# An eight-layer network on one core: layer 6 regrouped into 64-token chunks, weights centred ahead, attention's sums placed earlier in TensorE's queue

## The chip, the cores and the metric

The kernel runs on one core of a Trainium2 chip. The metric is the device time of one execution in microseconds (us). The core has five engines with a queue of instructions each: PE (TensorE, matmuls; PEld is its weight load), DVE (VectorE), ACT (ScalarE), POOL (GpSimd) and SP (SyncE, which issues DMAs). Each queue is worked off in order.

## What is computed

The reference takes `x` of 4 sequences x 1024 tokens x 128 columns through eight layers. After each, `x = layernorm(x + layer(x))`, without weight or bias:

```python
def _layernorm(x, axis=-1, eps=1e-05):
    m = jnp.mean(x, axis=axis, keepdims=True)
    v = jnp.var(x, axis=axis, keepdims=True)
    return (x - m) / jnp.sqrt(v + eps)
```

Layers 0 to 7 are: a similarity count with a linear map `W2` (0); a binarised feed-forward (1); attention in which, for every token and each of 16 heads, the 64 queries of the head attend to its 64 keys under a causal mask (2); a ternary feed-forward with an inner layer norm (3); a gated linear recurrence (4); four routed experts (5); a state-space layer (6); two Kronecker mixtures of experts with top-2 routing (7). Two of them matter here.

Layer 2, for each token and head, `softmax(mask(q k^T)) v` over 64 x 64 scores: by far the most elementwise work.

Layer 6 (16 heads, state 64, head width 8) works in chunks, and any chunk length gives the same result. With `A` the log decay of a token, `B` and `C` projections of 64 columns per head, `X` the scaled input:

```python
Lmat = jnp.exp(segsum(A))
Y_diag = jnp.einsum('bclhn,bcshn,bhcls,bcshp->bclhp', C, B, Lmat, X)
states = jnp.einsum('bclhn,bhcl,bclhp->bchpn', B, decay_states, X)
Y_off = jnp.einsum('bclhn,bchpn,bhcl->bclhp', C, states, state_decay_out)
```

## The kernel before

**Tiling and stages.** The 4096 tokens are 32 tiles of 128 tokens on the partitions. Layers 0 and 1 (`front`, line 1824) run over eight blocks of four tiles. Layer 2 runs over 64 units of 64 tokens, two per tile. Layers 3 to 7 run over nine groups (`SIZES`, line 27): seven of four tiles, two of two.

**Layer 2.** `prepare` (795) makes queries and masked maxima, `feed` (862) cuts each unit into 17 pieces of 128 to 1920 columns, and `rest` (917) finishes a piece. A piece goes round all engines: DVE multiplies queries by a key (903; two of the 17 on POOL), POOL subtracts the maximum (931), ACT exponentiates, PE adds up the denominators `den` (949), DVE multiplies in place by the value (954), PE adds up the numerators `num` (966). Pieces in flight lie in a ring of `ERING` = 8904 columns (line 33). `close` (986) divides (`rd<-num`, 992), and after each second unit multiplies by `Wo`, adds the residual and normalises the tile.

**Norms.** `norm` (549) ends layers 0, 1, 3, 4, 5 and 6: DVE adds the residual in PSUM (lines 635, 735, 1112, 1224, 1539; layer 5 adds it with its experts), `stats` (534) takes bn_stats and bn_aggr per tile on DVE, ACT makes the reciprocal deviation, and `shifts` (563) the shift; ACT then scales and shifts each tile, and `transpose` (572) turns it on PE. `close` has its own copy of this for one tile, whose last step is on DVE.

**Layer 6** (1313): per group, for each tile `j` and each quarter `hq` of the heads, `chunk` (1406) projects `B` and `C` of four heads into one bank, lays them in SBUF, makes the decay rows `em` (four ACT passes of 128 columns, a sum on PE in float32, an Exp), multiplies them with the products `C B` on DVE (two of 256 columns), and adds `X` weighted by them into the output bank (`within`, 1425). `across` (1460) adds the old state's part, transposes `B`, makes the new state's increment and updates the state on DVE (two of 8 columns). 128 such chunks in all. `drain` (1497) gates the output.

**Order.** All of it is one program in which a planner sets the order. Each stage is a generator that yields the engine it needs next; `Order.note` (173) adds up estimated durations (`length`, 85) and `Order.run` (249) always takes the step that can start first. Among steps of one engine that start within 0.05 us of each other, the rank decides (`URGE`, 1934, in `urge`, 240): `close` 0, `prepare` 1, the chains of the other layers 2, `rest` 3, `feed` 4; a chain that is ahead of the attention's pace gets 9. When attention is through, its rooms (ring, PSUM banks, query buffers) are handed to the other layers by `retire` (354) and the list `HEIRS` (1931). Every operation is recorded in one helper, so the profile shows line 61 for all; they are told apart by tile names.

The rank is read here:

```python
URGE = {"close": 0, "prepare": 1, "chain_a": 2, "chain_b": 2, "chain_c": 2, "rest": 3, "feed": 4}
```

Of the kernel before, what the change touches and what calls it, by code (L numbers as in the profile page):

```python
# [32 lines left out]
ERING = 8904  # L33
# [6 lines left out]
    "f2_bu": 1, "a3_bdt": 16, "a3_Alog": 16, "f3_sup": 1, "f3_sdn": 1, "bup": 64, "bdn": 32, "rep": 32, "SL": P, "U": P,  # L40
# [98 lines left out]
class Order:  # L139
# [100 lines left out]
    def urge(self, t):  # L240

        if t.rank in self.pace:
            group, steps, size = self.pace[t.rank]
            lag, total = LAG[t.rank]
            if group + size * min(1.0, steps / total) > self.place - (lag if group < HURRY else 0.0):
                return 9
        return self.rank[t.rank]
# [73 lines left out]
class Model:  # L321
# [4 lines left out]
    def __init__(self, ctx, tc, a):  # L326
# [13 lines left out]
            "x": (5, 512), "xT": (5, 512), "a": (6, 512), "b": (12, 512), "c": (4, 512), "gt": (1, 1024), "xp": (2, 152),  # L340
# [79 lines left out]
    def start(self):  # L420
# [23 lines left out]
        for i in range(3):  # L444
            self.d.dma_start(left[32 * i : 32 * i + 2], a["bias"])
        for i in range(3):
            self.v.tensor_copy(part, left[:66])
            self.v.tensor_copy(self.bias[32 * i : 32 * i + 2], part[32 * i : 32 * i + 2])
            self.v.tensor_tensor(left[:66], left[:66], part, ALU.subtract)
# [4 lines left out]
        self.d.dma_start(self.Wo, a["a1_Wo"].rearrange("(c p) d -> p c d", p=P))  # L454

# [7 lines left out]
        self.state = self.keep([P, 8, 32], "state")  # L463
# [3 lines left out]
        self.negA = self.keep([P, H], "negA")  # L467
# [5 lines left out]
        self.mask16 = self.keep([P, P], "mask16", dtype=BF16)  # L473
        self.v.tensor_scalar(self.mask16, self.k["SL"], -30000.0, None, ALU.mult)
# [73 lines left out]

    def norm(self, g, c, r):

        x = g.x
        mv, rs = yield from self.stats(r, c)
        nm = self.shifts(c, mv, rs)
        for j in range(g.n):
            self.s.activation(x[:, j, :], r[:, j, :], AF.Identity, scale=rs[:, j : j + 1], bias=nm[:, j : j + 1])
        self.drop(r)
        yield from self.transpose(g.xT, [x[:, j, :] for j in range(g.n)])
# [50 lines left out]
    def count(self, g, nT):  # L608
# [18 lines left out]
        w = yield from self.load("a", self.a["a0_W2"].rearrange("(c p) d -> p c d", p=P), 2, D)  # L627
# [6 lines left out]
        yield "DVE"  # L634
        self.v.tensor_tensor(po, g.x, po, ALU.add)
# [23 lines left out]
    def binarise(self):  # L659

        for half, n, count in ((0, 1, D), (1, 4, 512)):
# [22 lines left out]
            self.v.tensor_tensor(wT, wT, bw, ALU.add)  # L684
            self.drop(ab, bw, alpha)
# [4 lines left out]
            self.drop(wT)  # L690

# [17 lines left out]
    def layer1(self, g):  # L709
# [15 lines left out]
        for j in range(TPG):  # L725
# [3 lines left out]
            for f in range(4):  # L729
                self.pe.matmul(  # L730
                    po[:, j, :], lhsT=hT[:, f, j * P : (j + 1) * P], rhs=w2T[:, f * D : (f + 1) * D],
                    start=False, stop=(f == 3),
                )
        yield "DVE"
        self.v.tensor_tensor(po, g.x, po, ALU.add)
# [250 lines left out]
    def close(self, unit):  # L986
# [22 lines left out]
        if u == 1:  # L1009
# [10 lines left out]
            st, mv, rs = self.small([P, 6], "cst"), self.small([P, 2], "cmv"), self.small([P, 1], "crs")  # L1020
            self.v.tensor_tensor(po, x, po, ALU.add)
            self.v.bn_stats(st, po)
            self.v.bn_aggr(mv, st)
            yield "ACT"
            self.rstd(rs, mv[:, 1:2])
            yield "DVE"
            self.v.tensor_scalar(x, po, mv[:, 0:1], rs, ALU.subtract, ALU.mult)
# [10 lines left out]
    def ternarise(self):  # L1038
        self.w3 = []
        for half in range(2):  # L1040
# [18 lines left out]
            self.v.scalar_tensor_tensor(wT, wT, hi, neg, ALU.is_gt, ALU.subtract)  # L1059
            self.drop(pg, neg)  # L1060
# [5 lines left out]
    def layer3(self, g):  # L1066
# [37 lines left out]
        for j in range(n):  # L1104
            yield "PE"
            for f in range(4):
                self.pe.matmul(
                    po[:, j, :], lhsT=hT[f][:, j * P : (j + 1) * P], rhs=prT[:, f * D : (f + 1) * D],
                    start=(f == 0), stop=(f == 3),
                )  # L1110
        yield "DVE"
        self.v.tensor_tensor(po, g.x, po, ALU.add)
# [5 lines left out]
    def layer4(self, g):  # L1118
# [89 lines left out]
        Wo = yield from self.load("a", a["a2_Wo"], D)  # L1208
# [12 lines left out]
        for j in range(n):  # L1221
            self.pe.matmul(po[:, j, :], lhsT=og[:, j * P : (j + 1) * P], rhs=Wo, start=True, stop=True)
        yield "DVE"
        self.v.tensor_tensor(po, g.x, po, ALU.add)
# [4 lines left out]
    def layer5(self, g):  # L1229
# [4 lines left out]
        def fetch(e):  # L1234
# [3 lines left out]
            self.d.dma_start(ew[e][1], a["f2_W2"][512 * e : 512 * e + 512].rearrange("(c p) d -> p c d", p=P))  # L1238
# [74 lines left out]
    def layer6(self, g):  # L1313
        a, xT, n = self.a, g.xT, g.n
        SL, U = self.k["SL"], self.k["U"]
        yield "SP", self.free("b", 2)
        w, room = self.new("b"), self.new("b")
        X = room[:, : n * D].rearrange("p (j h q) -> p j h q", h=H, q=8)
        wbcs = {}

        def weights():
            for hq in range(4):
                yield "SP", self.free("b", 1 if n == TPG else 6)
                wbcs[hq] = self.new("b")
                for i, name in enumerate(("WB", "WC")):
                    self.d.dma_start(wbcs[hq][:, 256 * i : 256 * i + 256], a["a3_" + name][:, 256 * hq : 256 * hq + 256])
# [3 lines left out]
        self.d.dma_start(Wout, a["a3_Wout"])  # L1330
        Xf = X.rearrange("p j h q -> p j (h q)")

        little = room[:, n * D : n * D + 40 * n] if n < TPG else self.small([P, 40 * n], "little", bufs=1)
        dt, A = (little[:, 16 * n * i : 16 * n * (i + 1)].rearrange("p (j h) -> p j h", h=H) for i in range(2))
        over = little[:, 32 * n :].rearrange("p (j e) -> p j e", e=8)
# [5 lines left out]
        def inner(j):  # L1341
            yield "PE", self.free("bg")
            ps = self.new("bg")
            self.pe.matmul(ps[:, :144], lhsT=xT[:, j * P : (j + 1) * P], rhs=Wx, start=True, stop=True)
            yield "ACT"
            self.s.copy(Xf[:, j, :], ps[:, :D])
            yield "DVE"
            self.v.tensor_tensor(dt[:, j, :], ps[:, D : D + H], self.k["a3_bdt"], ALU.add)
            self.drop(ps)

        yield from self.together(*(inner(j) for j in range(n)))
        yield "ACT", self.free("bg")
        ps = self.new("bg")[:, : 2 * n * H].rearrange("p (i j h) -> p i j h", i=2, h=H)
# [3 lines left out]
        self.v.tensor_tensor(A, dt, self.negA[:, None, :].to_broadcast([P, n, H]), ALU.mult)  # L1357
        yield "DVE"
        self.v.tensor_tensor(X, X, dt[:, :, :, None].to_broadcast([P, n, H, 8]), ALU.mult)
# [4 lines left out]
        pa = ps[:, : 2 * n * H].rearrange("p (i j h) -> p i j h", i=2, h=H)  # L1364
        for i, m in enumerate((SL, self.ones)):
# [5 lines left out]
        for e in range(2):  # L1371
            rows = slice(64 * e, 64 * e + 64)
            self.s.activation(over[rows], pa[rows, 1].rearrange("p j (t e) -> p j t e", e=2)[:, :, :, e], AF.Exp)
        if n == TPG:
            dx = self.small([P, n, H, 8], "dx", bufs=1)
            yield "DVE"
        else:
            yield "DVE", self.free("b", 4)
            dx = self.new("b", n, H, 8)
        self.v.tensor_tensor(dx, X, pa[:, 0, :, :, None].to_broadcast([P, n, H, 8]), ALU.mult)  # L1380
# [18 lines left out]
        def add(t, jj, what, i, lhsT, rhs):  # L1399
            sums, done = bank(t)  # L1400
            done[i] += 1
            self.pe.matmul(
                sums[32 * i : 32 * i + 32, jj, what, :], lhsT=lhsT, rhs=rhs, start=done[i] == 1, stop=done[i] == 16
            )

        def chunk(j, hq):
            cols, at, hs = slice(j * P, (j + 1) * P), 4 * j + hq, slice(4 * hq, 4 * hq + 4)

            yield "PE", self.free(
                "bg", also=lambda: count["begun"] == at and hq in wbcs and min(moved) >= j - 1,  # L1410
                at=lambda: self.order.until(wbcs[hq]), b=3,
            )
            count["begun"] += 1
            bc, em, ps = self.new("b", 4, P), self.new("b", 4, P), self.new("bg", 4, P)
            wbc = wbcs[hq].rearrange("p (i c) -> p i c", c=P)
            for i in range(4):
# [641 lines left out]
```

## Time and profile before

| | |
|---|---|
| median of 3 runs | 3943.88 us (3942.16 to 3946.77) |
| the profiled execution | 3950.88 us |
| its span, first to last instruction | 3949.1 us |
| mean granted TensorE clock | 0.912 |
| chain that ended last, by engine | DVE 27%, PE 26%, POOL 15%, ACT 15%, issue 11%, DMA 5% |
| DMA | 331.30 MB, mean 84 GB/s |

A line of a group of instructions reads: engine, operation, output tile <- input tiles, shapes (partitions x elements), count | busy us, mean ns of one | idle us of the engine just before them, and what ended it. A line of waits reads: engine and tile that waited <- engine and tile that released it: us in total, times, longest. A window's line has its length and then each engine's busy us with its instructions.

### The profile page before, as it was taken

The numbers are of one execution on the slowest core, as the hardware profiler recorded it, in microseconds if no ns is written. First come the engines' busy times: TensorE is split into PE (matmuls) and PEld (weight loads), VectorE is DVE, ScalarE is ACT, GpSimd is POOL, SyncE is SP. The second block draws the span as 40 slices with busy tenths as digits, with TensorE's granted clock in tenths as the row PEclk, the third lists the DMA queues.
The fourth block names the chain that finished last, engine by engine and source line by source line (L and its number), as shares of the span: only waits on it lengthen the run. The fifth ranks groups of instructions, "written<-read, shape, count | busy, mean of one in ns | idle before, by whom it ended". The sixth has DMA issues, their size and how long they took to land.

```text
span 3949.1 us, 128735 instructions
## 1 busy us (share of the span) xinstructions
PE 3099.8 (78%) x55472; PEld 1614.1 (41%) x55472; DVE 3258.2 (83%) x4477; ACT 2612.3 (66%) x4970; POOL 2921.3 (74%) x1320
## 2 busy tenths in 40 slices
PE   6676677777788887978888887887878887879883
PEld 2232223333344453544444543544434443436562
DVE  3878999899998879989988789999998998893421
ACT  5576575666677785677667775777657776666541
POOL 1879996899789777879778787798888986791000
PEclk8788888988999998999999999999999999999986
DMA  3221222212224134233433324343432334234565
GB/s 90 58 50 44 47 64 53 60 44 49 52 66 115 51 90 105 66 109 83 100 84 79 101 63 97 80 121 79 101 75 62 105 81 122 71 86 117 163 154 118
DMA packets 385297, 331.30 MB, mean 84 GB/s; under 512 B 196108, under 2 KB 320460, under 8 KB 384728
## 3 DMA queue, kind: packets, MB, share of 16 engines
q1 hardware_dynamic: 375384, 289.53, 29.6%
q0 software_dynamic: 9344, 33.56, 2.9%
q8 instruction: 434, 7.11, 0.8%
q14 instruction: 135, 1.11, 0.1%
HBM read 147.85 MB, written 40.89 MB: 48 GB/s over the span
## 4 chain that ended last, share of the span: by engine, by line
DVE 27%; PE 26%; POOL 15%; ACT 15%; issue 11%; DMA 5%; SPq 1%; DVEq 0%; POOLq 0%; ACTq 0%
DVE ringe L61 17%; POOL ringe L61 15%; PE bg L61 14%; ACT ringe L61 7%; PE den L61 6%; DVE bg L61 5%; PE num L61 4%; PE kvr L61 2%; ACT b L61 1%; ACT ha L61 1%; SPq L61 1%; ACT L61 1%; DVE a L61 1%; DVE b L61 1%; ACT t L61 1%
## 5 line engine op out<-in xcount | busy, mean ns | idle before, releaser
L61 POOL TENSOR_TENSOR ringe<-ringe,mr 128x1024 f32<-128x1024 f32 (+14 forms) x1088 | 2557.1, 2384 | 459.1 <-DVE ringe L61 342.5
L61 DVE TENSOR_TENSOR ringe<-ringe,kvr 128x1024 f32<-128x1024 f32 (+14 forms) x1094 | 1288.0, 1207 | 188.8 <-PE den L61 168.0
L61 ACT ACTIVATE ringe<-ringe 128x768 f32<-128x768 f32 (+14 forms) x962 | 999.5, 1056 | 580.5 <-POOL ringe L61 578.6
L61 DVE TENSOR_TENSOR ringe<-qr,kvr 128x1024 f32<-128x1024 f32 (+12 forms) x960 | 1102.0, 1184 | 33.9 <-PE num L61 24.5
L61 PE MATMUL den<-ringe,cst 128*32 128x256 f32 (+7 forms) x8712 | 697.8, 416 | 263.7 <-ACT ringe L61 230.0
L61 PE MATMUL num<-ringe,cst 128*32 128x256 f32 (+7 forms) x8712 | 698.6, 407 | 245.8 <-DVE ringe L61 239.3
L61 PEld LDWEIGHTS num<-ringe,cst 128*32 128x32 f32 x8712 | 227.1, 113 | 585.9 <-DVE ringe L61 458.3
L61 PEld LDWEIGHTS den<-ringe,cst 128*32 128x32 f32 x8712 | 232.9, 114 | 571.5 <-ACT ringe L61 365.5
L61 ACT ACTIVATE ringe<-ringe,cst 128x256 f32<-128x256 f32 x512 | 357.4, 781 | 60.9 <-POOL ringe L61 60.8
L61 POOL TENSOR_TENSOR ringe<-qr,ks 128x896 f32<-128x896 f32 (+1 forms) x128 | 286.9, 2241 | 88.3 <-PE num L61 66.0
L61 PE MATMUL bg<-xT,a 128*32 128x512 f32 (+1 forms) x1868 | 249.4, 629 | 30.5 <-DVE a L61 12.1
L61 PE MATMUL kvr<-wkv,xT 128*32 128x256 f32 x2048 | 148.9, 412 | 35.7 <-DVE ringe L61 31.0
L61 DVE TENSOR_TENSOR_SCAN bg<-ends,bg 128x512 f32<-128x512 bf16 x128 | 155.1, 1216 | 25.2 <-PE bg L61 25.2
L61 PE MATMUL bg<-a,ha 128*32 128x128 f32 x4672 | 164.4, 285 | 13.7 <-ACT ha L61 13.7
L61 ACT COPY b<-bg 128x256 f32<-128x256 f32 (+2 forms) x224 | 99.6, 452 | 94.3 <-PE bg L61 82.2
L61 PEld LDWEIGHTS bg<-a,ha 128*32 128x32 f32 x4672 | 131.0, 115 | 35.0 <-ACT ha L61 17.5
L61 PE MATMUL bg<-xT,b 128*32 128x128 f32 (+1 forms) x3448 | 127.8, 290 | 6.4 <-DVE state L61 3.5
L61 ACT ACTIVATE b<-cst,little 128x128 f32<-128x128 f32 x416 | 132.0, 395 | 0.0
L61 DVE TENSOR_TENSOR b<-b,bg 128x256 f32<-128x256 f32 (+1 forms) x252 | 97.4, 419 | 27.6 <-PE bg L61 22.9
L61 ACT ACTIVATE ha<-bg,cst 128x512 f32<-128x512 f32 (+1 forms) x152 | 98.8, 674 | 31.8 <-PE bg L61 30.5
L61 PE MATMUL bg<-b,cst 128*32 128x512 f32 x864 | 116.7, 606 | 1.8 <-ACT b L61 1.4
L61 PEld LDWEIGHTS bg<-xT,b 128*32 128x32 f32 x3448 | 102.4, 115 | 36.2 <-issue 17.1
(681 smaller groups left out, 4405.2 us busy)
## 6 DMA issues: line engine op xcount, KB each, us to landing
qr<-q SPq DMA_DIRECT2D x512, 128.0 KB
mr<-t SPq DMA_DIRECT2D x512, 128.0 KB
a<-in_f_W SPq DMA_DIRECT2D x65, 256.0 KB
c<-in_f_Wdn SPq DMA_DIRECT2D x54, 256.0 KB
c<-tu SPq DMA_DIRECT2D x196, 64.0 KB
tu<-gt SPq DMA_DIRECT2D x24, 512.0 KB
c<-td SPq DMA_DIRECT2D x92, 128.0 KB
td<-gt SPq DMA_DIRECT2D x22, 512.0 KB
```

Of the source, the lines that this page charges most:

```text
L61: return f(*args, **kw)
```

## The change

- **Layer 6** takes chunks of 64 tokens. The two halves of the partitions hold two heads (even and odd, by a reordering of the weights on the host), so a tile of 128 tokens is two chunks `c` with two heads `e`; `chunk(j, b)` now covers eight heads, and 64 of them make the layer. `B` and `C` have a bank each. The products, the transposition (a matmul by the identity), the increments, the old state's part and the outputs are matmuls on 64 x 64 or 64 x 32 corners of the array, sixteen of each per chunk. The decay rows are eight ACT passes of 64 columns, the decay product is one DVE instruction of 512 columns, and the state is updated twice per chunk, by a multiplication and an addition of 32 columns each.
- **Centred weights.** `centre` takes from each row of a final weight its mean over the 128 outputs, so that a layer's output has mean zero (`x` has it already). It is applied once to the weights and biases that end layers 0 to 6; those that are loaded again and again go to DRAM and back (`levelled`). A norm is then only a scaling: `level` squares on ACT with an accumulator and scales on ACT. The residual comes in by a matmul with the identity (by an identity in `W2` in layer 0); in `close` and layer 5 DVE still adds it.
- **Order**: `rest` on PE, that is the sums `den` and `num`, has the rank of `prepare`.
- **Rooms**: the ring has 8368 columns, `xp` 448 instead of 152, `state` 56 per head pair instead of 32.

```diff
-ERING = 8904
+ERING = 8368
...
+        if t.rank == "rest" and t.engine == "PE":
+            return self.rank["prepare"]
         return self.rank[t.rank]
...
+    def centre(self, w, n):
+
+        rows = w.partition_size()
+        w = w.rearrange("p (c d) -> p c d", c=n)
+        s = self.small([P, 8], "mean", bufs=1)[:rows, :n]
+        self.v.tensor_reduce(s, w, AX.X, ALU.add)
+        self.v.tensor_scalar_mul(s, s, 1.0 / D)
+        self.v.tensor_tensor(w, w, s[:, :, None].to_broadcast([rows, n, D]), ALU.subtract)
+
+    def level(self, x, r, rs):
+
+        n = r.shape[1]
+        for j in range(n):
+            self.s.activation(x[:, j, :], r[:, j, :], AF.Square, accum_out=rs[:, j : j + 1])
+        self.s.activation(rs, rs, AF.Ln, scale=1.0 / D, bias=self.eps)
+        self.s.activation(rs, rs, AF.Exp, scale=-0.5)
+        for j in range(n):
+            self.s.activation(x[:, j, :], r[:, j, :], AF.Copy, scale=rs[:, j : j + 1])
+
     def norm(self, g, c, r):
 
-        x = g.x
-        mv, rs = yield from self.stats(r, c)
-        nm = self.shifts(c, mv, rs)
-        for j in range(g.n):
-            self.s.activation(x[:, j, :], r[:, j, :], AF.Identity, scale=rs[:, j : j + 1], bias=nm[:, j : j + 1])
+        x, rs = g.x, self.small([P, TPG], c + "rs")[:, : g.n]
+        yield "ACT"
+        self.level(x, r, rs)
...
-        w = yield from self.load("a", self.a["a0_W2"].rearrange("(c p) d -> p c d", p=P), 2, D)
+        w = yield from self.load("a", self.level_w["a0_W2"][0], 2, D)
...
+    def levelled(self, *names):
+
+        for name in names:
+            src = self.a[name].rearrange("(e c p) d -> e p c d", p=P, c=min(4, self.a[name].shape[0] // P))
+            self.level_w[name] = []
+            for e in range(src.shape[0]):
+                n = src.shape[2]
+                w = yield from self.load("a", src[e], n, D)
+                yield "DVE"
+                if name == "a0_W2":
+                    self.v.tensor_tensor(w[:, 0, :], w[:, 0, :], self.ident, ALU.add)
+                self.centre(w.rearrange("p c d -> p (c d)"), n)
+                yield "SP"
+                put_by = self.keep([P, n * D], name, pool=self.dram)
+                self.d.dma_start(put_by, w.rearrange("p c d -> p (c d)"))
+                self.level_w[name].append(put_by)
+                self.drop(w)
...
-        yield "DVE"
-        self.v.tensor_tensor(po, g.x, po, ALU.add)
+            self.pe.matmul(po[:, j, :], lhsT=g.xT[:, j * P : (j + 1) * P], rhs=self.ident, start=False, stop=True)
...
-            st, mv, rs = self.small([P, 6], "cst"), self.small([P, 2], "cmv"), self.small([P, 1], "crs")
+            rs = self.small([P, 1], "crs")
             self.v.tensor_tensor(po, x, po, ALU.add)
-            self.v.bn_stats(st, po)
-            self.v.bn_aggr(mv, st)
             yield "ACT"
-            self.rstd(rs, mv[:, 1:2])
-            yield "DVE"
-            self.v.tensor_scalar(x, po, mv[:, 0:1], rs, ALU.subtract, ALU.mult)
+            self.level(x[:, None, :], po[:, None, :], rs)
...
+            def decay():
                 yield "ACT"
                 for i in range(4):
-                    self.s.activation(em[:, i, :], U, AF.Identity, scale=A[:, j, 4 * hq + i : 4 * hq + i + 1])
+                    for c in range(2):
+                        at = 2 * j + c
+                        self.s.activation(em[:, i, c], U, AF.Identity, scale=A[:, at, 4 * b + i : 4 * b + i + 1])
...
+            yield from self.together(made(B, wbcs[b][0]), made(C, wbcs[b][1]), decay())
...
+                pg = self.new("bg", 4, 2, C2)
                 for i in range(4):
...
+                    for c in range(2):
+                        for e in range(2):
+                            self.pe.matmul(
+                                pg[half(e), i, c], lhsT=part(B, i, c, e), rhs=part(C, i, c, e), start=True, stop=True
+                            )
...
-                for i in range(2):
-                    self.v.tensor_tensor(ev[:, i], ev[:, i], pg[i], ALU.mult)
+                self.v.tensor_tensor(em, em, pg, ALU.mult)
...
+                def old(c):
+                    for i in range(4):
+                        for e in range(2):
+                            add(j, c, 1, e, b, self.state[half(e), 4 * b + i, 24 - 8 * i : 56 - 8 * i], part(C, i, c, e))
+
+                def new(c):
+                    s = self.state[:, hs, 24:32]
+                    self.v.tensor_tensor(s, s, over[:, 2 * j + c, hs, None].to_broadcast([P, 4, 8]), ALU.mult)
+                    self.v.tensor_tensor(s, s, got[:, c], ALU.add)
+
...
+                            self.pe.matmul(
+                                ps[half(e), i, c], lhsT=part(B, i, c, e), rhs=self.ident[half(e), half(e)],
+                                start=True, stop=True,
+                            )
+                old(0)
+                yield "ACT"
+                self.s.copy(B, ps.rearrange("p i c s -> p i (c s)"))
+                yield "PE"
...
+                                got[half(e), c, i], lhsT=part(B, i, c, e), rhs=dx[half(e), 2 * j + c, 4 * b + i],
+                                start=True, stop=True,
+                            )
+                yield "DVE"
+                new(0)
+                yield "PE"
+                old(1)
                 if not last:
...
                     yield "DVE"
+                    new(1)
...
         yield from self.front(self.blocks[0])
         yield from self.front(self.blocks[1])
         yield from self.ternarise()
+        yield from self.levelled("a2_Wo", "f2_W2", "a3_Wout")
...
+            self.order.spawn(self.levelled("a0_W2"), "chain_a")
             self.order.spawn(self.binarise(), "chain_a")
```

## The prediction

> **What bounds the kernel now.** I read the page's busy times first, then the windows of all engines, cut where a unit of attention ends, then the waits, then the groups of VectorE by shape.
>
> ```profile
> PE 3099.8 (78%) x55472; PEld 1614.1 (41%) x55472; DVE 3258.2 (83%) x4477; ACT 2612.3 (66%) x4970; POOL 2921.3 (74%) x1320
> ```
>
> No engine is full over the span, but the span has three parts. The first attention product (`ringe<-qr,kvr`, line 903) starts at 87.9 us, and the last unit's division (`rd<-num`, line 992) at 3577.2 us. In between DVE is busy 3124.4 us of 3489 (89.5%), POOL 2889.6, PE 2774.8, ACT 2405.3. After it come 372 us in which the last groups run through layers 3 to 7. The 64 divisions mark units of equal attention work; here are the first seven stretches of eight units, with the columns length, PE, PEld, DVE, ACT, POOL, clock, DMA:
>
> ```profile
> 157.00:552.00 395.00, 272.01 (x3676) 107.93 (x3668) 340.80 (x363) 251.30 (x395) 353.78 (x157) 0.84 0.22 51
> 552.00:961.00 409.00, 312.18 (x4732) 142.63 (x4732) 371.82 (x438) 263.58 (x435) 355.99 (x154) 0.89 0.22 54
> 961.00:1404.00 443.00, 361.05 (x6204) 180.76 (x6208) 398.33 (x527) 321.62 (x611) 368.46 (x168) 0.93 0.28 70
> 1404.00:1842.00 438.00, 362.80 (x6708) 190.63 (x6700) 397.98 (x539) 311.09 (x570) 355.05 (x155) 0.95 0.36 90
> 1842.00:2313.00 471.00, 389.55 (x7140) 214.71 (x7136) 409.46 (x565) 338.76 (x659) 369.30 (x168) 0.93 0.34 87
> 2313.00:2745.00 432.00, 354.57 (x6644) 186.87 (x6635) 397.59 (x530) 306.22 (x562) 361.73 (x161) 0.96 0.37 92
> 2745.00:3175.00 430.00, 352.98 (x6405) 180.89 (x6404) 396.61 (x533) 293.17 (x545) 360.49 (x160) 0.94 0.35 87
> ```
>
> POOL does the same work in each stretch. What grows is the other layers' work, and the length with it: from the first stretch to the mean of the last five, the length goes from 395 to 442.8 us, DVE from 340.8 to 400.0, PE from 272.0 to 364.2. If the whole rise is put on DVE, 1 us of it costs 47.8/59.2 = 0.81 us; if on PE, 47.8/92.2 = 0.52. POOL's 354 us for eight units is a floor far below.
>
> ```profile
> POOL ringe L61 <- DVE ringe L61: 342.5, 105, 23.4
> DVE ringe L61 <- PE den L61: 168.3, 142, 4.8
> POOL ringe L61 <- PE num L61: 98.5, 17, 13.7
> ```
>
> POOL mostly waits for DVE; DVE waits mostly for TensorE's `den` sums, since it overwrites their operand; the ring's space (waits on `num`) is third.
>
> **The change, part by part.** First DVE:
>
> ```profile
> L61 DVE TENSOR_TENSOR b<-b,bg 128x256 f32<-128x256 f32 x245 | 92.7, 412 | 27.6 <-PE bg L61 22.9 <-PE den L61 2.9 <-ACT b L61 1.2
> L61 DVE SCALAR_TENSOR_TENSOR state<-state,little,bg 128x8 f32<-128x8 f32 x186 | 32.2, 213 | 6.1 <-ACT b L61 3.3 <-PE bg L61 2.8
> L61 DVE TENSOR_TENSOR bg<-x,bg 128x512 f32<-128x512 f32 x37 | 25.4, 687 | 32.9 <-PE bg L61 32.9
> L61 DVE BATCH_NORM_STATS2 ast<-bg 128x6 f32<-128x128 f32 x82 | 22.5, 274 | 0.7
> L61 DVE BATCH_NORM_AGGREGATE amv<-ast 128x2 f32<-128x6 f32 x104 | 18.9, 182 | 3.6
> L61 DVE TENSOR_SCALAR x<-bg,cmv,crs 128x128 f32<-128x128 f32 x31 | 12.5, 404 | 3.6 <-ACT crs L61 3.6
> ```
>
> - Norms of layers 0, 1, 3, 4, 5, 6 over 32 tiles: 192 bn_stats x 0.275 and 192 bn_aggr x 0.182 go, 87.7 us; the residual adds (37 of 512 columns, 6 of 256) go, 27.9. In `close` 32 bn_stats x 0.299, bn_aggr x 0.182 and scalings x 0.404 go, 28.3.
> - Layer 6's decay product: 256 of 256 columns (105.5 us) become 64 of 512 at 0.671 (42.9): -62.6.
> - Its state: 224 x 0.215 = 48.2 us become 240 tensor_tensors of 32 columns. Rows of 16 and 64 columns take 0.163 and 0.205; I take 0.19: 45.6, so -2.6.
> - Centring the weights once: some 3,700 columns, each reduced and subtracted (512 columns: 0.678 and 0.692) and small ones: +16, nearly all beside the feed or ahead of it.
>
> DVE's sum: -193 us. The instruction lists of both kernels say the same: 4461 instructions become 3796. Some 52 of the 256 decay products and an eighth of the norms come after 3577 us, so within the feed -168 us (49 + 77 + 24 + 27 + 2 - 11).
>
> ACT: the shifts (192 x 0.284, 52 x 0.189) go, -64; the normalising pass drops its bias, 0.444 to 0.389 (row `a<-x,rn`), 192 times, -11; squares with their accumulator read (0.298 + 0.190) come, 224 times, +109, and 32 passes in `close`, +12. Layer 6: 512 decay rows of 128 columns x 0.395 become 512 of 64; between 0.264 (4 columns, one pointer) and 0.395, I take 0.33, -33; 64 of the 128 Exp, -38; evictions 128 x (0.579 + 0.368) become 192 x 0.579, -10; smaller ones -15. Sum -50 us; ACT was 69% busy, so I count nothing.
>
> PE (a quarter chunk is 128 tokens by four heads, a half chunk by eight): a float32 matmul shows two records (2,048 for the 1,024 of `kvr<-wkv,xT`), so twice busy/records is one instruction. A quarter chunk now: 16 projections x 0.071, mask 4 x 0.106, decay sum 4 x 0.272, products 4 x 0.207, state 4 x 0.112, 4 x 0.109, two transposes x 0.233, 8 of 8 columns x 0.038: 5.13 us, x 128 = 657. After: 32 projections, mask and decay sum as before (3.78 us) and 80 small matmuls (16 each of products, transposition by the identity, old state, new state, output). Nothing here runs that form in layer 6; layer 7's 64x64 tiles take 0.077 (`bg<-c,hc`: 25.2 us, 656 records). Lower bound 0.038 (8 columns), upper 0.112 (64x128). I take 0.077, the same tile and columns: 9.94 us x 64 = 636, -21; bounds -220 to +158. The identity adds for the residual in layers 1, 3, 4 and 6, 512 x 0.071 = +36. Sum +15, bounds -184 to +194.
>
> A price that speaks against it: matmuls of layer 6 change the array's shape, and `PEld bg` loses 378.4 us to "issue" in 1,096 waits, 0.35 us each. Three odd-shaped blocks per quarter chunk before (384), at most six per half chunk after (6 x 64 = 384): nothing added. The Trainium skill's TensorEngine Tiling (Array Packing), Key Properties, states that a change of tiling mode drains the engine; if each of the 384 blocks cost two such waits of 0.35 us, 270 us would be paid before and after alike; the trace does not name the cause of these waits, so it neither shows nor denies that.
>
> SP: per group of layer 6, eight weight loads become four of twice the size; seven loads and seven stores for the centred weights come early; its list goes from 1,883 to 1,861. The early ones stand ahead of the third and fourth block's `x`, which the feed reaches only at 961 us; without that cover it would cost their length once: six rounds of two transfers at 2.3 us (`a0_W2`, issued 29.1, used 31.4) and 1.5 us of centring, some 37 us.
>
> Startup: the centred `a0_W2` goes to DRAM and back, queued on SP behind the four `wkv` bias rows; layer 0's matmuls wait for it. Against it, the norm's way from the last matmul to the scaled tile took 5.9 us (35.0 to 40.9) and now has 4 x 0.49 + 0.5 + 1.5 = 4.0. Two norms, -4, the round trip about +2: -2, bounds -6 to +8.
>
> The ring is 6% smaller: its waits (98.5 on POOL, 24.5 on DVE) grow by 6%, +7, bounds 0 and +123. `den` and `num` now go ahead of the other layers on PE: DVE's 168 us for `den` can shrink; bounds 0 and -168. The 142 waits average 1.2 us, and one piece's sums of 256 columns alone take 129.0/192 = 0.67 us, so most of a wait is not the turn; I take an eighth, -21. In DVE's list the runs of foreign instructions between two attention products shrink from 1.00 to 0.73 on average, which goes the same way.
>
> New waits: within a chunk, the second half's old-state matmuls wait for DVE's update of the first; behind them on PE stand `den`, `num` and the projections. Twice 64 such waits replace 128 single ones: nothing counted, price below.
>
> Tail: DVE's list leaves about the same for after the last unit (15 half chunks of layer 6, where 26 quarter chunks stood); four norms per group some 2 us shorter: -8, bounds -25 to +10.
>
> **Sum:** feed 168 x 0.81 = -136, ring and order -14, tail -8, startup -2: -160. The profiled execution took 3950.9 us (span 3949.1), 7 us over the median; from the median, 3943.9 - 160 = **3784**.
>
> **Rivals.**
> - *DVE's time is worth less.* From the first to the second stretch 31.0 us more DVE cost 14 us, 0.45. Then 168 gives 76, the tail little: **3865**. For it: PE and ACT are not relieved. Against: later stretches cost more per us.
> - *It is worth all of it.* DVE keeps 89.5%: 168/0.895 = 188, and `den`'s early turn takes half of 168 as well: some -270, **3675**. POOL then fills 89%, as it did in the first stretch.
> - *Slower: PE's queue becomes the choke.* Small matmuls at 0.112 add 194 us, and the 128 waits in the middle of a chunk, at 1.4 us each (`PEld bg` waits on `DVE a`: 44.0 us, 31 times), 182 more; 376 x 0.52 = 196 us against 160 gained: **3980**. It decides from 160/0.52 = 308 us of new PE time. Against: it needs the upper bound and every wait bare.
> - *The work does not go.* The lists show it gone; only a gain that the order eats stays, within 0.2% of before (about what a measurement can tell from no change).
>
> **Chances:** forecast (3735 to 3835) 0.50, worth less (3835 to 3936) 0.20, worth all (under 3735) 0.14, no change 0.04, choke 0.12. Range 3680 to 3940, which leaves out the choke, no change's upper part and the quickest third of "worth all"; faster 0.84, same 0.04, slower 0.12.
>
> **What would show it.** Right: DVE's busy time near 3065, units near 52 us apart (54.3 now), `DVE ringe <- PE den` below 168, the tail near 364. Wrong: units as far apart as now with PE busier by over 150 us (the choke), or DVE's share falling below 87% while its work went (worth less); a later first product would show the round trip.

## The result, and the profile after

The changed kernel takes 3958.97 us (median of 20 runs), the kernel before 3945.45 (20 runs): ratio 1.0038, 95% interval 1.0030 to 1.0046. It is a little slower, where 3784 was forecast. The page of its profiled execution (3955.8 us, span 3953.9) begins:

```profile
PE 3121.0 (79%) x61008; PEld 1761.9 (45%) x61008; DVE 3242.1 (82%) x3812; ACT 2563.8 (65%) x5005; POOL 2921.6 (74%) x1320
```

DVE has 665 instructions fewer, and is busy 16 us less instead of 193. The windows up to the last unit's division (3556.8 us) and after it, with the columns length, PE, PEld, DVE, ACT, POOL, clock, DMA:

```profile
88.00:3557.00 3469.00, 2788.16 (x52763) 1505.56 (x52758) 3136.09 (x3482) 2364.22 (x4409) 2895.20 (x1283) 0.93 0.33 82
3557.00:3954.00 397.00, 281.57 (x7691) 231.71 (x7681) 88.30 (x287) 157.16 (x488) 21.86 (x24) 0.83 0.42 109
```

Units are 54.0 us apart (54.3 before), and what comes after the last one takes 397 us (372 before). The groups of DVE instructions show where the work went:

```profile
L61 DVE TENSOR_TENSOR state<-state,little 128x32 f32<-128x32 f32 x106 | 130.3, 1230 | 14.6 <-PE num L61 13.4 <-PE bg L61 1.2
L61 DVE TENSOR_TENSOR state<-state,bg 128x32 f32<-128x32 f32 x107 | 20.0, 187 | 21.1 <-PE bg L61 10.2 <-ACT enm L61 2.3 <-ACT b L61 1.4
L61 DVE TENSOR_TENSOR a<-a,mean 128x512 f32<-128x512 f32 x6 | 11.3, 1879 | 0.2
L61 DVE TENSOR_SCALAR mean<-mean 128x4 f32<-128x4 f32 x6 | 11.0, 1825 | 0.2
```

The first two rows are the two halves of one state update, with the same 32 columns. The second reads `bg`, in PSUM, and takes 0.187 us; the first has all operands in SBUF and takes 1.23 us on the mean, from 0.156 to 8.319. Centring shows the same: four columns cost 1.825 us. The timeline tells what such an instruction waits for (start, length, engine; an entry with x2 is two instructions in a row). DVE, then POOL:

```profile
894.77 3.18 DVE L61 TENSOR_TENSOR state<-state,little 128x32 f32<-128x32 f32 x1
898.09 0.19 DVE L61 TENSOR_TENSOR state<-state,bg 128x32 f32<-128x32 f32 x1
```

```profile
890.21 7.70 POOL L61 TENSOR_TENSOR ringe<-ringe,mr 128x1792 f32<-128x1792 f32 x2 [2.28 <-DVE ringe L61]
897.86 2.77 POOL L61 TENSOR_TENSOR ringe<-qr,ks 128x1536 f32<-128x1536 f32 x1
```

POOL's pair ends at 897.91 us and the multiplication at 897.95. Once POOL is idle the same instruction is short: in the 150 us after the last unit POOL is busy for 0 us, and the 16 multiplications of the first row that lie there take 0.156 to 0.193 us, as here:

```profile
3577.34 0.18 DVE L61 TENSOR_TENSOR state<-state,little 128x32 f32<-128x32 f32 x1
3577.56 0.19 DVE L61 TENSOR_TENSOR state<-state,bg 128x32 f32<-128x32 f32 x1
```

Behind a multiplication that waits, DVE's next attention product stands still, and PE, whose next matmuls read the state:

```profile
PEld bg L61 <- DVE state L61: 65.3, 39, 7.4
PE bg L61 <- DVE state L61: 46.4, 30, 6.5
```

These two rows were 22.8 us before. They overlap, since a weight load and its matmul wait for the same update: behind the multiplication shown above, both go on at 898.33 us. The Trainium skill, SBUF — State Buffer, Who interferes with whom, states that a VectorE instruction with two SBUF inputs contends with a GpSimd instruction that reads SBUF, for a port pair that is an exclusive lock; this trace agrees, with 1.23 us against 0.187.

### The profile page after: what moved, and what is told of

Its sections match the earlier page's. It is cut to its first block, busy times and chain, and to the rows that moved or that the text cites. A ratio compares the mean times of both kernels' runs of the same rounds, so it can differ in the third digit from the quotient of the medians.

```text
span 3953.9 us, 138772 instructions
## 1 busy us (share of the span) xinstructions
PE 3121.0 (79%) x61008; PEld 1761.9 (45%) x61008; DVE 3242.1 (82%) x3812; ACT 2563.8 (65%) x5005; POOL 2921.6 (74%) x1320
## 4 chain that ended last, share of the span: by engine, by line
PE 31%; DVE 29%; ACT 14%; POOL 12%; issue 9%; DMA 4%; SPq 1%; DVEq 0%; POOLq 0%; ACTq 0%
DVE ringe L61 18%; PE bg L61 16%; POOL ringe L61 12%; PE den L61 7%; ACT ringe L61 6%; PE num L61 6%; DVE bg L61 4%; PE kvr L61 3%; DVE state L61 3%; ACT ha L61 1%; SPq L61 1%; DVE a L61 1%; ACT b L61 1%; ACT x L61 1%; ACT L61 1%
## 5 line engine op out<-in xcount | busy, mean ns | idle before, releaser
L61 POOL TENSOR_TENSOR ringe<-ringe,mr 128x1024 f32<-128x1024 f32 (+14 forms) x1088 | 2556.9, 2386 | 481.2 <-DVE ringe L61 357.3
L61 ACT ACTIVATE ringe<-ringe 128x1664 f32<-128x1664 f32 (+14 forms) x966 | 999.3, 1054 | 601.2 <-POOL ringe L61 599.4
L61 PE MATMUL bg<-a,ha 128*32 128x128 f32 x4672 | 155.1, 275 | 11.0 <-ACT ha L61 10.6
L61 ACT COPY b<-bg 128x512 f32<-128x512 f32 (+1 forms) x185 | 96.1, 533 | 76.3 <-PE bg L61 75.3
L61 DVE TENSOR_TENSOR state<-state,little 128x32 f32<-128x32 f32 x106 | 130.3, 1230 | 14.6 <-PE num L61 13.4
L61 PE MATMUL bg<-xT,b 128*32 128x128 f32 x3624 | 132.6, 293 | 4.0 <-DVE bg L61 1.6
L61 PEld LDWEIGHTS bg<-xT,a 128*32 128x32 f32 x1888 | 59.5, 116 | 125.6 <-issue 58.7
```

Source lines behind the costliest of these rows:

```text
L61: return f(*args, **kw)
```

## The experiments

Theory 1: such VectorE instructions wait for POOL, and ate the gain. Theory 2: the rank of `rest` and the room for the ring change the order, and more of the other layers comes after the last unit. Rival: TensorE's queue, with its small matmuls, is the choke.

All runs in one table: median time, ratio to the kernel before with its 95% interval, DVE's busy time, the feed (first to last division), the tail (last division to the end of the span), and PE's busy time in the tail. The columns behind the ratio are of the profiled execution. The kernel before ran again beside each set of runs, with medians from 3945 to 3954 us, and the ratios go by these; differences of the times in the text carry that scatter.

| | us | ratio | DVE | feed | tail | PE in tail |
|---|---|---|---|---|---|---|
| before | 3945 | | 3258 | 3420 | 372 | 267 |
| after | 3959 | 1.0030–1.0046 | 3242 | 3400 | 397 | 282 |
| e1 after, decays in PSUM | 3902 | 0.9869–0.9899 | 3138 | 3356 | 395 | 284 |
| e2 after, no rank | 3994 | 1.0111–1.0144 | 3237 | 3456 | 373 | 257 |
| e3 before, state update in SBUF | 4200 | 1.0636–1.0670 | 3505 | 3624 | 413 | 291 |
| e4 before, rank | 3968 | 1.0039–1.0067 | 3259 | 3318 | 494 | 352 |
| e5 before, norms | 3887 | 0.9830–0.9867 | 3166 | 3336 | 383 | 288 |
| e6 before, layer 6 with decays in PSUM, ring 8176 | 3952 | 1.0002–1.0022 | 3219 | 3438 | 341 | 241 |
| e7 = e1, no rank | 3969 | 1.0040–1.0071 | 3131 | 3360 | 438 | 313 |
| e8 = e1, rank only early | 3925 | 0.9931–0.9963 | 3136 | 3390 | 380 | 266 |
| e9 = e1, raw W2 at first | 3878 | 0.9804–0.9837 | 3140 | 3348 | 392 | 279 |
| e10 = e5, rank | 3926 | 0.9928–0.9958 | 3169 | 3252 | 510 | 371 |
| e11 before, ring 8368 | 4014 | 1.0154–1.0186 | 3262 | 3447 | 406 | 277 |
| e12 = e1, pace constant | 3921 | 0.9916–0.9946 | 3139 | 3345 | 426 | 310 |
| e13 = e9, ring 8904 | 3842 | 0.9699–0.9733 | 3134 | 3290 | 405 | 304 |
| e14 = e13, no rank | **3825** | 0.9655–0.9688 | 3124 | 3325 | 346 | 243 |
| e15 = e6, ring 8904 | 3888 | 0.9825–0.9863 | 3215 | 3392 | 332 | 232 |
| e16 after, ring 8904 | 3960 | 1.0009–1.0030 | 3261 | 3380 | 427 | 312 |
| e17 = e14, residual on DVE | 3841 | 0.9715–0.9742 | 3148 | 3366 | 317 | 219 |
| e18 before, ring 8704 | 3924 | 0.9924–0.9951 | 3256 | 3397 | 364 | 261 |

### The state update

e1 copies the decays into free columns of the increment's bank, so that the multiplication has an operand in PSUM:

```diff
                 def new(c):
-                    s = self.state[:, hs, 24:32]
-                    self.v.tensor_tensor(s, s, over[:, 2 * j + c, hs, None].to_broadcast([P, 4, 8]), ALU.mult)
+                    s, k = self.state[:, hs, 24:32], fade[:, c]
+                    self.v.tensor_tensor(s, s, k[:, :, None].to_broadcast([P, 4, 8]), ALU.mult)
...
                 self.s.copy(B, ps.rearrange("p i c s -> p i (c s)"))
+                fade = ps.rearrange("p i c s -> p (i c s)")[:, 64:72].rearrange("p (c i) -> p c i", c=2)
+                self.s.copy(fade, over[:, 2 * j : 2 * j + 2, hs])
```

> The changed kernel, with one operand moved: ACT copies the eight decays of a chunk into unused columns of the increment's bank (64 more small ACT passes, about 13 us), so the state's multiplication reads one operand from PSUM. The number, shapes and order of VectorE's instructions stay. Theory 1 (an instruction of VectorE whose operands all lie in SBUF waits while POOL works): the row of state multiplications falls from 1.23 us to about 0.19, VectorE's busy time by 110 us, and PE's waits for the state (112 us in two rows) mostly go; at 0.8 us per us of VectorE that is 3959 - 88 = about 3870, between 3850 and 3900. Rival (TensorE's queue with its many small matmuls is the choke and VectorE's waits lie beside it): the row falls too, but the time moves by under 25 us, to 3935 or more. Rival (it is the strided state, or the broadcast decay, that is slow): the row stays at 1.2 us and the time at 3959.

e3 goes the other way, in the kernel before:

```diff
-                        self.v.scalar_tensor_tensor(
-                            s, s, over[:, j, 2 * hq + pr : 2 * hq + pr + 1], ps[:, 2 + pr, :8], ALU.mult, ALU.add
-                        )
+                        k = over[:, j, 2 * hq + pr : 2 * hq + pr + 1].to_broadcast([P, 8])
+                        self.v.tensor_tensor(s, s, k, ALU.mult)
+                        self.v.tensor_tensor(s, s, ps[:, 2 + pr, :8], ALU.add)
```

> The kernel before, whose 224 state updates (one instruction with an operand in PSUM, 0.215 us) become a multiplication with both operands in SBUF and an addition with one in PSUM. Theory 1: the multiplications take about 1.2 us on the mean although they have 8 columns, those after the feed 0.16; VectorE's busy time grows by some 220 us and the time by 0.8 of that, to about 4100 (4040 to 4150). Rival (instructions of this size cost their columns and no more): 224 additions of about 0.16 us more, 36 us on VectorE and 29 us of time, 3975.

Measured: e1 3902, e3 4200. The state's groups and PE's waits for it, e1 first, then e3:

```profile
L61 DVE TENSOR_TENSOR state<-state,bg 128x32 f32<-128x32 f32 x222 | 41.1, 185 | 56.6 <-PE bg L61 34.3 <-PE kvr L61 8.0 <-PE num L61 5.8
...
PEld bg L61 <- DVE state L61: 9.9, 16, 1.7
PE bg L61 <- DVE state L61: 3.3, 4, 1.5
```

```profile
L61 DVE TENSOR_TENSOR state<-state,little 128x8 f32<-128x8 f32 x200 | 258.2, 1291 | 0.0
...
PEld bg L61 <- DVE state L61: 144.4, 52, 7.2
PE bg L61 <- DVE state L61: 116.9, 48, 6.3
```

Theory 1 holds on both sides: with the operand in PSUM both halves take 0.185 us; eight columns without one take 1.29, as long as 32 do, so it is not the size. In e3 DVE is busy 247 us more and the kernel 252 us slower. In e1 DVE's 104 us less and PEld's 55 us less of waiting for the state (PE's 43 overlap with these) gave only 57 us, less than the 88 expected. Of the 48 us between the two profiled executions, 45 lie in the feed.

### The parts

e5 is the kernel before with the norms, centred weights and identity matmuls alone; e6 is layer 6 alone (decays in PSUM; the old norms' buffers need room, so the ring has 8176); e7 is e1 without the two lines of the rank.

> The kernel before with the centred weights and the norms without mean alone (identity matmuls for the residual with them); layer 6, the ring and the rank as before. The prediction's sum for this part: VectorE loses 87.7 + 27.9 + 28.3 - 16 = 128 us, 11 of them after the feed, at 0.81: 95 us, 3850. What the traces of before and after make of it now: VectorE loses some 100 us (the bn rows counted overlap twice, centring costs 33), and TensorE gains 54 us of identity adds (0.109 each); at the 0.5 to 0.7 us that the state's repair gave back for each us of VectorE this is 3880 to 3900. Rival (TensorE's and ScalarE's additions eat it): within 10 us of 3947.

> The changed kernel's layer 6 alone, with the decays in PSUM as in the first run of this study; norms and rank as before, ring 8176 columns since the old norms' small buffers need room. The prediction's sum: VectorE loses 65 us, 3900 with some 10 us for the ring. Theory (what the half chunks take from VectorE they give to TensorE's queue: 16 more weight loads per kind, and a wait on VectorE in the middle of each chunk): 3945 to 3985, with PEld busier by 150 us and DVE's waits for PE's bg longer. Rival (layer 6 is as good as predicted and the rest eats it): 3890 to 3910.

> The changed kernel with the decays in PSUM and without the rank of rest on PE: together with the two runs before it, whether the parts add up. If the rank is worth 35 us here as it was in the changed kernel: 3937. If norms alone give about 50 and layer 6 alone costs about 25: 3925. If the rank only moves work past the last unit, as it did in the kernel before: 3890.

Measured: 3887, 3952 and 3969. Norms are worth 58 us, as the traces' count of e5 had it; layer 6 nothing with its ring of 8176 columns (7 lost; with the ring of before, in e15 below, 57 gained); and both together lose 24, which none of the three expectations of e7 had. The feeds nearly add up (84 us less by e5, 18 more by e6: 3354; e7 has 3360). The tails don't: +11 and -31 would give 352, and e7 has 438.

### The rank

e2 takes the rank's two lines out of the changed kernel, e4 puts them into the kernel before, e10 into e5, and e8 keeps them in e1 until attention's fifth group of eight (`and self.place < HURRY`).

> The changed kernel without the line that ranks rest on PE with prepare: den and num come after the other layers again. Theory 2 (the early sums hold the other layers back, so more of them is left after attention): layer 6 of the seventh group starts earlier before the last unit than now (91 us), the 397 us after the last unit fall to about 370, the units stay 54.0 us apart or become up to 0.5 us longer, DVE's wait for den stays near 166 us; 3930 to 3950. Rival (the early sums are worth what was predicted, 21 us or more of the feed): the feed grows by 20 us or more and the time stays or rises, 3955 to 3985. Rival (the tail is longer because of layer 6's own new instructions): the tail stays within 8 us of 397.

> The kernel before with the rank of rest on PE alone changed. As predicted: an eighth of DVE's wait for den (168 us) goes and the time falls by about 21 us, to 3924. Theory 2: the feed gets at most that, and the 372 us after the last unit grow by 20 us or more because the other layers come later; 3940 to 3965. Rival (no effect either way): within 8 us of 3945, units and tail as before.

> Norms alone, with the rank of rest on PE. Theory (the rank moves the other layers behind the attention: less feed, more tail): the feed falls by 40 to 100 us and what comes after the last unit grows by as much or more, 3885 to 3910. Rival (the rank is worth 35 to 65 us wherever VectorE has been relieved, as in the changed kernel with and without the repair): 3825 to 3855.

> The changed kernel with the decays in PSUM and the rank of rest on PE only until the attention has passed its fifth group of eight. Theory (the rank shortens the feed by holding the other layers back, and what is held back at the end comes after the last unit): the feed keeps most of its gain, the time after the last unit falls from 395 to about 375, 3885 to 3895. Rival (the order at the end does not decide the tail): 3902 or more.

Measured: 3994, 3968, 3926, 3925. The rank shortens the feed by 102 us in the kernel before, 84 on e5, 55 in the changed kernel. It lengthens the tail by 122, 127 and 24. So theory 2 was right there in what it does and wrong in the sum: in the changed kernel the rank is worth 35 us, so that e2 became slower, not faster. It does not hold in all pairs: from e7 to e1 the rank shortens the feed by only 4 us, and the tail by 43 instead of lengthening it; why stays open. e10 and e8 missed their ranges, too. The windows of e10, up to its last division and after it:

```profile
88.00:3410.00 3322.00, 2677.31 (x46779) 1344.12 (x46767) 3006.04 (x3488) 2354.67 (x4379) 2884.61 (x1271) 0.93 0.31 77
3410.00:3920.00 510.00, 371.30 (x9171) 267.19 (x9170) 146.10 (x456) 231.25 (x726) 33.06 (x36) 0.85 0.54 139
```

PE does 84 us less in the first and 83 more in the second than in e5 (2761, 288): work is moved, none is saved. And in all twenty kernels the tail is PE's busy time in it and 95 to 142 us more; a line through them rises by 1.26 us of tail per us of PE. That what is left to PE sets the tail's length fits this, but no run tests it by itself. e8 shortened the tail by 15 us and gave back 34 in the feed.

### The start

In the changed kernel the first attention product comes at 102.05 us, where it came at 87.94. SP's queue in it:

```profile
18.69 0.33 SPq L61 DMA_DIRECT2D a<-in_a_Wkv  x1
19.11 0.38 SPq L61 DMA_DIRECT2D a_W<-a  x1
19.54 0.28 SPq L61 DMA_DIRECT2D wq<-in_a_Wq_b  x1
24.96 14.50 SPq L61 DMA_DIRECT2D wkv<-in_a_Wkv_b  x4
39.64 0.35 SPq L61 DMA_DIRECT2D a<-a_W  x1
```

`a_W<-a` stores the centred W2, `a<-a_W` loads it for layer 0: 39.6 us, where the load stood at 29.1. In front of it stand the store and the four bias rows of `wkv`, issued from 24.96 to 39.46 us. Behind it come layer 1's binarised weights, and they are later still: the loads `a<-w` are issued at 55.92 us where they were at 36.08, and layer 1's first matmul waits for them until 58.77 us (42.09 before). SP, then PE:

```profile
41.33 0.43 SPq L61 DMA_DIRECT2D a<-in_f_w2T  x1
55.43 0.32 SPq L61 DMA_DIRECT2D w<-a  x1
55.92 1.88 SPq L61 DMA_DIRECT2D a<-w  x2
```

```profile
58.77 5.71 PE L61 MATMUL bg<-xT,a 128*32 128x512 f32 x32 [8.31 <-DMA a<-w]
```

e9 lets the first two blocks of layer 0 take the uncentred W2 and the old norm:

> The changed kernel with the decays in PSUM, in which the first two blocks of layer 0 take the uncentred W2, with the residual added on VectorE and a norm with the mean, as the kernel before does; the centred W2 is made later, for the other six blocks. Theory (the way of the centred W2 to DRAM and back holds SP's queue: layer 0's load is issued at 39.6 us where it was at 29.1, and the first attention product comes at 101 us where it came at 88): the first product returns to 88 to 90 us, the time falls by 8 to 13 us against the first run of this study, 3890. Rival (other work fills the start, and the feed is set by what follows): the first product is early, and the time stays within 4 us of 3902.

```profile
92.15 7.61 DVE L61 TENSOR_TENSOR ringe<-qr,kvr 128x1024 f32<-128x1024 f32 x9 [0.22 <-issue]
```

Measured: 3878, better than the 3890 expected. The first product is 9 us earlier than in e1, the first division 9.7; the first product stays 4 us later than before. The rest of the gain, 11 us between the profiled executions, lies in the feed and the tail, and is not explained by the start.

### The ring, and the order

e11 gives the kernel before the smaller ring alone; e12 sets the constant that turns layer 6's steps into progress for the planner from 290 to 235 in e1; e13 and e14 give the ring its 8904 columns back in e9, with and without the rank (the zeros between the windows of `xp` and of the state are shared, `[P, 8, 32]` for `[P, 8, 56]`); e15 does so with e6 (one room for `xp`); e16 with the changed kernel itself; e18 tries 8704 in the kernel before.

> The kernel before with a ring of 8368 columns. As predicted: the waits for the ring's space (98.5 us on POOL, 24.5 on DVE) grow by 6%, 7 us: 3954. Rival (the ring is what eats the gain of the whole change, since the norms alone with the full ring are at 3887 and all parts with the small one at 3969): 3990 or more. Rival (no effect): within 5 us of 3947.

> The changed kernel with the decays in PSUM, and with the constant that turns layer 6's steps into progress set from 290 to 235: its half chunks need 253 to 257 steps a group where the quarter chunks needed 310 to 323, and the constant was left. Theory (the pacing sees layer 6 further back than it is, serves it early and others late): the tail of 395 us falls, 3880 to 3895. Rival (it makes layer 6 wait more, and more of it comes after attention): tail 400 or more, 3905 to 3925.

> The ninth run's kernel (decays in PSUM, raw W2 for the first two blocks) with the ring of 8904 columns again: the windows of xp and of the state share their zeros (256 columns each in place of 448), which makes the room. Theory (the smaller ring cost 69 us alone, and costs the like here): 3878 less 40 to 70, 3810 to 3840. Rival (the ring's price in the kernel before was an accident of the planned order, and does not carry over): 3865 to 3890, or more.

> As the thirteenth run, without the rank of rest on PE. With the rank, norms alone became 38 us slower and the kernel before 20 us slower, both with the full ring; with the small ring it was worth 35 and 67 us. Theory (the rank is worth something only where the small ring keeps VectorE waiting; with the full ring it moves work behind the attention): 20 to 40 us faster than the thirteenth run, 3790 to 3820. Rival (the rank helps the new layer 6): 30 us or more slower than the thirteenth run.

> Layer 6 alone as in the sixth run, with the full ring (8904 columns; one room for xp instead of two gives the space, at the cost of a wait now and then). Theory (in the sixth run the ring's price hid layer 6's gain): 3952 less 40 to 70, 3880 to 3910, which is what the prediction had for this part. Rival (layer 6's half chunks are worth nothing, whatever the ring): 3935 to 3960.

> The changed kernel with the ring of 8904 columns alone (xp and state packed to make the room; state update with all operands in SBUF, start and rank as changed). If the ring's price stands by itself, as it did in the kernel before (69 us), in layer 6 alone (64) and in the ninth against the thirteenth run (37): 3959 less 35 to 70, 3890 to 3925. Rival (the state's waits hide it): 3945 or more.

> The kernel before with a ring of 8704 columns: room for the eight pieces 384 to 1536 around a unit's first large one (8704 together), but not for the six of 1792 to 1152 (8832), which 8904 has and 8368 has not. Theory (what counts is which runs of pieces fit, and the six large ones are the greater loss): 3985 to 4015. Rival (the price goes with the columns, 0.129 us for each): 3947 + 26 = 3973. Rival (any other order costs as much as it happens to): anything else, below 3965 or above 4020.

Measured: 4014, 3921, 3842, 3825, 3888, 3960, 3924. e11 cost 69 us where 7 were predicted, and after e13 (37 us back) and e15 (64 back) the ring seemed to be what was missing. e16 and e18 speak against that: the full ring gives the changed kernel nothing (feed 20 us shorter, tail 30 longer, and the state's multiplications, at 1.48 us, cost 26 us more), and a ring of 8704 is 22 us *faster* than one of 8904. In e11 DVE's busy time is that of before, and the two rows of waits for the ring's space (`num` on POOL and DVE) are 127 us against 123; nothing in them is 69 us long; 27 us of the loss lie in the feed, 34 in the tail. Each size gives the planner another order, and the same work then takes 3924 to 4014 us. What 536 columns cost for themselves can't be told from these runs, and stays open. e12's rival was right: 19 us slower. e14, 16 us faster than e13, fell short of its theory's 20 to 40: without the rank the feed is 35 us longer and the tail 59 shorter. And e15 has the matmuls of e6 in 64 us less, so they are not what kept layer 6 from its gain in e6, as the theory there had it.

### The residual on TensorE

e17 adds the residual on DVE again in layers 1, 3, 4 and 6 of e14.

> The fourteenth run's kernel, with the residual added on VectorE again in layers 1, 3, 4 and 6 in place of the identity matmuls: VectorE gains some 22 us (32 instructions of 0.687), TensorE loses 54 (496 at 0.109). As predicted (VectorE decides, TensorE's us cost nothing): 15 to 18 us slower, 3840. Rival (TensorE's work is worth as much, above all after the last unit, where it is over 90% busy): within 8 us of 3825, or faster.

Measured: 3841, 16 us slower, as the prediction's way of counting has it (DVE +24 us). By the scatter below it could be an accident of the order.

## Why the prediction was wrong, step by step

**What bounds the kernel: not contradicted. The price of DVE's time, 0.81: near, but not shown.** DVE stayed busy for 90% of the feed. A line through the twenty kernels' time and DVE's busy time rises by 0.79 us per us (0.64 without e3), and they lie 38 us (standard deviation) beside it. The two runs that changed little but the waits of DVE give 0.55 (e1, 57 us for 104) and 1.02 (e3, 252 for 247).

**DVE's sum: wrong, -16 us for -193; this is the step that failed.** Of the 177 us:
- 110 are the state's 240 instructions: 155 us, predicted 45.6. The 0.19 us came from rows with an operand in PSUM, and no row with all operands in SBUF was looked for. The 0.163 and 0.205 were `little<-bg,cst` and `little<-bg,negA`. The trace of before had such a row: two equal instructions on SBUF alone, each with one input and a column of scalars. The first began while a pair of POOL's ran, which ended at 149.28 us, and ended at 149.57; the second began just after POOL's instruction of 162.15 to 164.51:

```profile
147.62 1.95 DVE L61 TENSOR_SCALAR a<-a,ter_lo 128x512 f32<-128x512 f32 x1
...
164.53 0.48 DVE L61 TENSOR_SCALAR a<-a,ter_lo 128x512 f32<-128x512 f32 x1
```

- 24 are the centring (33.5 for 16) and layer 3's ternary weights (11.7 for 5.2), for the same reason.
- The remaining 43 are in the means. Short DVE instructions overlap, and busy time counts the overlap once. In the trace of before:

```profile
666.96 0.27 DVE L61 BATCH_NORM_STATS2 ast<-bg 128x6 f32<-128x128 f32 x1
667.26 0.18 DVE L61 BATCH_NORM_AGGREGATE amv<-ast 128x2 f32<-128x6 f32 x1
667.36 0.27 DVE L61 BATCH_NORM_STATS2 ast<-bg 128x6 f32<-128x128 f32 x1
```

These entries overlap. From tile to tile it is 0.40 us, not 0.275 + 0.182: 192 of them are 77 us, not 87.7. Two decay products take 0.74, not 0.824: 128 pairs are 11 us less. The other 21 are not split.

This step explains why the change is no gain: with its largest term repaired and nothing else changed, e1 is 1.2% faster than the kernel before. It is not all of the miss. Of the 175 us between 3784 and 3959, e1 brought back 57. With the start, the ring and the rank changed as well, e14 has DVE busy 134 us less than before; at 0.79 that is 106, and 120 were measured. The runs do not divide the other 118 us of the miss cleanly, since each variant is another order as well.

**ACT -50: right** (2612 to 2564). **PE +15: right in size** (3099.8 to 3121.0); the small matmuls took 0.068 to 0.081 us for 0.077, the identity adds 0.109 for 0.071. **New waits on PE in the middle of a chunk, counted at nothing: wrong in the changed kernel** (39 waits of PEld for the state, 1.7 us each), and nearly right once the multiplication no longer waits (16 of 0.6 us in e1). The choke's 1.4 us per wait was thus met, but for 39 waits where it had 128, and for another reason than the matmuls. It is not the mechanism: with these matmuls, and that wait mostly gone, e14 is 120 us faster than before.

**Startup -2, bounds -6 to +8: wrong.** +14 us at the first product; the store and load were priced as a round trip, not with what they do to the other transfers of the start; the last to come was layer 1's weights, 20 us later than before. e9 shows that the centred W2, with the norm that goes with it, brought 9 of the 14 us; which link of it (room, queue or order) is not split.

**`den` and `num` first, -21: wrong in sign by case.** DVE's wait for `den` hardly moved:

```profile
DVE ringe L61 <- PE den L61: 165.7, 154, 7.9
```

It was 168.3 before. The feed got shorter because other work was put off; what it is worth ranged from 38 us lost (e5 to e10) to 67 gained (e7 to e1). It lost in all three pairs with a ring of 8904 columns and gained in both with 8368; why is open.

**Ring +7: open. Tail -8: wrong, +25.** The tail was counted as the same work, less the norms; but PE was left with 282 us of work in it, where it had 267, and across the runs the tail goes with that work.

## What to carry to other kernels

Before counting an elementwise instruction by its columns, look where its operands lie: with all of them in SBUF, beside a busy POOL, even eight columns cost 1.3 us here and 32 cost 1.2, and moving one operand of the latter to PSUM by a small ScalarE copy took that to 0.19. Multiply short instructions by their distance in the timeline, not by their mean length. And where a planner sets the order, the same work in another order moved this kernel by 20 to 70 us: a gain of that size belongs to the part that was changed only if several variants show it.

## What the runs showed of the hardware that was not expected

- The instruction with all operands in SBUF loses, POOL does not: POOL's subtractions take 2557.1 us before and 2556.9 after. It does not always get in between two POOL instructions: the longest wait, 8.32 us from 1473.07, outlasts three of 1920, 1792 and 1664 columns, which run from 1469.40 to 1481.34. A scaling of one column (`mean<-mean 128x1`) took 0.15 us while an instruction of POOL ran (at 196.70 us, within POOL's 194.81 to 197.98); the six of four columns, with one input in SBUF, took 1.825 on the mean, and the one of them that ran while POOL was idle (at 54.51 us) took 0.17.
- In the 150 us after the last unit PE is 92 to 99% busy (47.0, 45.8 and 49.5 us of each 50), DVE 21 to 38% and ACT 58 to 71%. Over the whole tail it is 71%. TensorE, 79% busy over the span and behind DVE there, is the busiest engine in the tail.
